# A mixture-of-experts layer whose router runs once per quarter of the positions, with a region of rows for each expert

## The chip, the cores and the metric

The kernel runs on one core of one Trainium2 chip. A core has five engines that run at the same time, each with an instruction queue of its own: TensorE (PE; its weight loads are shown as PEld), VectorE (DVE), ScalarE (ACT), GpSimd (POOL) and SyncE (SP), and 16 DMA engines that they share. The metric is the device time of one execution in microseconds. The kernel before took 1349.56 us (median of three runs, 1344.41 to 1350.19).

## The reference, cut to what matters

The input `x` has 16 sequences of 256 positions and 128 channels, 4096 rows in all. Four layers follow each other, each on the layernorm of `x` and added to `x`:

```python
x = x + attn_a(layernorm(x))   # 16 heads of 8, within blocks of 64 positions of a sequence
x = x + ffn(layernorm(x))
x = x + attn_b(layernorm(x))   # 16 heads of 8, over the 16 sequences at each position
x = x + ffn(layernorm(x))

def ffn(x):                                  # the same weights both times
    logits = flat_x @ Wr                     # 8 experts
    top_vals, top_idx = jax.lax.top_k(logits, 2)
    rw = softmax(top_vals)
    combine = sum(rw[..., None] * one_hot(top_idx, 8), axis=1)
    g, u = einsum('nc,ech->neh', flat_x, Wg), einsum('nc,ech->neh', flat_x, Wu)
    eo = einsum('neh,ehc->nec', silu(g) * u, Wd) * DEPTH_SCALE   # hidden 512
    return einsum('ne,nec->nc', combine, eo)
```

So each row needs just two of eight experts. Which two, and how many rows an expert gets, is known only at run time.

## The kernel before, in words

**Tiling.** The 256 positions are cut into four quarters of 64 (`NQ`), each held on chip as a tile `xq[q]` of 128 partitions by 8 groups (`NG`) by 128 channels; a group is two sequences. Two quarters make a half (`NH` = 2, `QH` = 2 quarters each): 2048 rows (`TH`), of which each goes to two experts. A *stage* `s` is the expert layer on one half: stages 0 and 1 are the first expert layer on halves 0 and 1, stages 2 and 3 the second.

**Attention.** `attention_a` and `attention_b` work on one quarter: a layernorm with transposes to the channel-major form (`layernorm_t`; its `pow` for the reciprocal deviation is L235, on POOL), queries and keys, and then group by group the scores (L329, L415), the maximum and difference on DVE, the exponential on ACT (L343, L436), transposes, the product with the values (L360, L453) and the division. `attention_a` ends a group with two additions on POOL (L367, L368).

**Router.** `router(s)` takes the two quarters of a half together (16 groups, `GH`). It makes their layernorm, which is kept in `rows` along with the weight and the destination of each row (132 numbers of 4 bytes), the logits, the two largest of eight (`largest`), the weights, and then the place of each row among the rows of its expert: a running sum over the groups, products with a triangle and with ones (`rank`, `count`). The number of rows of each expert in the half is rounded up to tiles of 256 (`TT`), from `over` to `base`; an expert's rows begin where the tiles of the expert before end. `of_i` says for each of 23 tiles (`NT`) which expert it belongs to. Finally 32 indirect DMAs on POOL (L621), one for each group and choice, scatter 128 rows each to their places in `sorted_in[s]` in DRAM, which has 5888 rows.

**Fill.** Since no expert fills its last tile, `sorted_in[s]` is first written with zeros whose destination is out of the way (`fill`, one DMA on ACT's queue for each stage, L210).

**Experts.** `experts()` walks over 4 x 23 tiles. `fetch` reads the tile's 256 rows (`xin`) from fixed places of `sorted_in[s]`, loads the expert's number into a register of SP and reads its three weight matrices with it. A tile is two steps (pairs of hidden chunks): products L719 for `g` and `u`, tanh on ACT (L724), two operations on DVE (L725, L727), the product back (L670) one step later, and at the end the transposes (L681), the scaling by the row's weight on ACT (L686, `y`), the destination on DVE (L691, `to`) and two indirect DMAs on POOL (L693) that scatter 256 result rows into `results[s]`. `xin`, `w`, `y` and `to` have three buffers each. Rows that no one filled get a destination behind all real rows: `to` is the smaller of the destination read and a constant of the tile, `pads`.

**Combine.** `combine(s)` reads the results of a half back in order and adds them to `xq` (L747, L753).

**What sets the order.** The program writes `attend("a", 0)` (both quarters' attention and the router of stage 0) first, then the fills of stages 1 to 3, then the stages. In stage `s` the tiles' 46 steps are written interleaved with `beside(s)`: the combine of the stage before, then attention on the other half and its router. `rate` says how many steps of the side are written after each step of the tiles; the divisor 0.8 makes the side end after 80% of them. `ROUTER`, `STEPS_A`, `STEPS_B` count the side's steps. This written order is a priority: a planner places each instruction on its engine's queue, earlier written ones first, with later ones where an engine would stand idle. On the chip each queue then runs in its order.

Of the kernel before, what the change touches and what calls it, by code (L numbers as in the profile page):

```python
# [10 lines left out]
F32 = mybir.dt.float32  # L11
# [8 lines left out]
P = 128  # L20
# [8 lines left out]
CH = 512  # L29
# [20 lines left out]
K_ONE, K_TRI, K_STEP, K_LOW, K_NUM, K_DEST, K_PAD, K_END = 204, 332, 460, 468, 532, 556, 588, 634  # L50
# [4 lines left out]
def _constants():  # L55
# [28 lines left out]
    c[:, K_PAD : K_PAD + 2 * NT] = pad.reshape(P, 2 * NT)  # L84
    return c
# [3 lines left out]
def hybrid_kernel(  # L89
# [23 lines left out]
    p2 = ctx.enter_context(tc.tile_pool(name="p2", bufs=2))  # L113
    p3 = ctx.enter_context(tc.tile_pool(name="p3", bufs=3))
# [71 lines left out]
    number = k_sb[0:1, K_NUM : K_NUM + NT]  # L186

    rows = [const.tile([P, GH, TOP, RW], F32, name=f"rows{i}") for i in range(1)]
    for t in rows:
        nc.gpsimd.memset(t[:, :, :, C + 1 : RW], 0.0)  # L190
        nc.gpsimd.tensor_copy(
            t[:, :, :, C + 1],
            k_sb[:, K_DEST : K_DEST + TOP * GH].rearrange("p (g k) -> p g k", k=TOP),
        )

    runs = [const.tile([P, NG + GH, NE], F32, name=f"runs{i}") for i in range(2)]
# [3 lines left out]
    sorted_in = [dram.tile([NT * TT, RW], F32, name=f"sorted_in{s}") for s in range(NS)]  # L200
# [4 lines left out]
    nc.gpsimd.memset(zero[:, C + 1 : C + 2], float(TOP * TH + NT * TT))  # L205
# [3 lines left out]
    def fill(s):  # L209
        done = nc.scalar.dma_start(  # L210
            out=sorted_in[s].rearrange("(n p) r -> p n r", p=P),
            in_=zero.unsqueeze(1).to_broadcast([P, NT * TT // P, RW]),
        )
        before[s] = done.ins

    fill(0)

# [267 lines left out]
    def router(s):  # L485
        hf, layer = s % NH, s // NH + 1
        n = f"F{layer}{hf}"
        row = rows[0]
        pl = psum(f"lg_{n}")
        for qq in range(QH):  # L490
            q = QH * hf + qq
            lnT = p1.tile([P, TQ], F32, tag="lnF", name=f"ln_{n}_{qq}")

            def put(half, pt):
                nc.scalar.copy(lnT[:, half * CH : (half + 1) * CH], pt)

            def keep(g):
                return row[:, qq * NG + g, 0, 0:C]

            yield from layernorm_t(q, f"{n}_{qq}", put, keep)  # L500
            for g in range(NG):
                gg = qq * NG + g
                nc.tensor.matmul(
                    pl[:, gg * NE : (gg + 1) * NE],
# [337 lines left out]
```

## Time and profile before

| | |
|---|---|
| median of three runs | 1349.56 us |
| the profiled execution's own time | 1348.74 us |
| its span, first to last instruction | 1346.9 us |
| mean granted TensorE clock | 0.816 |
| PE / weight loads / DVE / ACT / POOL busy | 79% / 58% / 49% / 28% / 29% |
| DMA | 132.97 MB, 99 GB/s on the mean |
| first tile's first product (L719) | 278.67 us |
| first tanh of stages 1, 2 and 3 | 592.9, 886.4 and 1186.9 us |

The profile is of one execution. Times in it count from the first instruction. A line of a group says the code line, engine, operation and what it writes and reads (out<-in), then the busy time, the mean of one in ns, and the idle time just before, with what ended it. A line of the timeline gives start and duration in us, then the same, with the idle time in brackets. "ACTq" or "SPq" is the engine's sequencer, which issues DMAs. The granted clock is a share of TensorE's full speed.

### The profile page before, as it was taken

The page shows a single profiled execution, that of the slowest core. Times are in us where ns is not written, and L with a number is a line of the kernel's source. Part 1 is how long each engine was busy: PE and PEld are TensorE (multiplying, and loading weights), DVE is VectorE, ACT ScalarE, POOL GpSimd, SP SyncE. Part 2 cuts the span into 40 slices and gives each one's busy share as a digit, 9 for nine tenths or more (in the row PEclk, how much of TensorE's full clock was granted, in tenths as well). Part 3 has the DMA queues.
Part 4 walks back from the last instruction along what each step waited for, and adds up shares of the span by engine and source line. Part 5 has one row for each costly group of instructions (what it writes and reads, how often), then busy time and mean ns, then how long its engine had stood idle before and what let it go on. Part 6 is the DMA issues. An engine that isn't in the chain of part 4 may idle for free.

```text
span 1346.9 us, 22348 instructions
## 1 busy us (share of the span) xinstructions
PE 1059.1 (79%) x8280; PEld 775.2 (58%) x8280; DVE 655.1 (49%) x1760; ACT 377.3 (28%) x789; POOL 385.8 (29%) x461
## 2 busy tenths in 40 slices
PE   2798995079999998187999985578999985499992
PEld 0565665056766676063675763455766764378882
DVE  3435444045566645047657662157557651255443
ACT  0212221022333332022333431123333421133441
POOL 1001003712222214724112127423121127432331
PEclk9556555588898989586999997688899988699996
DMA  9900000321232323242332332261231332276563
GB/s 251 211 1 1 1 1 17 109 65 61 85 93 65 95 64 105 81 146 77 92 93 73 96 110 80 91 207 41 81 109 63 99 93 82 89 226 215 187 188 105
DMA packets 140635, 132.97 MB, mean 99 GB/s; under 512 B 12016, under 2 KB 111856, under 8 KB 140528
## 3 DMA queue, kind: packets, MB, share of 16 engines
q1 hardware_dynamic: 105920, 97.79, 24.5%
q0 software_dynamic: 9984, 20.73, 4.6%
q10 hardware_dynamic: 24624, 13.03, 4.5%
q8 instruction: 66, 1.08, 0.3%
q14 instruction: 41, 0.34, 0.1%
HBM read 96.26 MB, written 35.24 MB: 98 GB/s over the span
## 4 chain that ended last, share of the span: by engine, by line
PE 54%; another core or an unknown queue 6%; DVE 5%; POOL 4%; DMA 4%; issue 4%; ACT 2%; SPq 0%; ACTq 0%; POOLq 0%; DVEq 0%
PE g L719 11%; PE u L719 11%; PE acc L670 10%; PE sc_A L329 3%; PE sc_B L415 3%; POOL sorted_in L621 2%; PE o_A L360 2%; PE o_B L453 2%; DMA results<-yo,to 2%; PE xt L662 2%; PE y L681 2%; PE t_A L349 1%; PE t_B L442 1%; PE v_B L275 1%
## 5 line engine op out<-in xcount | busy, mean ns | idle before, releaser
L693 POOL DMA_INDIRECT results<-yo,to x184 | 178.2, 969 | 513.5 <-ACT yo L686 480.0
L719 PE MATMUL g<-xT,w 128*128 128x256 f32 x736 | 220.1, 418 | 39.0 <-issue 38.1
L670 PE MATMUL acc<-h,w 128*128 128x256 f32 x736 | 209.1, 403 | 25.3 <-DVE h L727 25.0
L725 DVE SCALAR_TENSOR_TENSOR th<-th,g 128x512 f32<-128x512 f32 x184 | 125.6, 683 | 201.7 <-ACT th L724 122.6
L719 PE MATMUL u<-xT,w 128*128 128x256 f32 x736 | 212.7, 409 | 2.1 <-DVE th L725 2.1
L724 ACT ACTIVATE th<-g 128x512 f32<-128x512 f32 x184 | 109.9, 597 | 341.4 <-PE g L719 212.9
L719 PEld LDWEIGHTS g<-xT,w 128*128 128x128 f32 x736 | 143.1, 205 | 82.4 <-issue 62.9
L670 PEld LDWEIGHTS acc<-h,w 128*128 128x128 f32 x736 | 141.1, 201 | 57.0 <-DVE h L727 34.4
L727 DVE TENSOR_TENSOR h<-th,u 128x512 f32<-128x512 f32 x184 | 125.8, 684 | 76.3 <-PE u L719 27.2
L719 PEld LDWEIGHTS u<-xT,w 128*128 128x128 f32 x736 | 142.2, 205 | 27.4 <-issue 5.1
L621 POOL DMA_INDIRECT sorted_in<-rows,pos_i_F x128 | 122.8, 959 | 44.2 <-issue 37.2
L329 PE MATMUL sc_A<-kA,qA 32*64 32x256 f32 x512 | 108.5, 537 | 16.5 <-DVE ex_A L337 15.2
L360 PEld LDWEIGHTS o_A<-va,eT_A 128*64 128x64 f32 x1024 | 79.4, 181 | 30.2 <-ACT eT_A L353 15.9
L336 DVE TENSOR_REDUCE mx_A<-sc_A 128x4 f32<-128x256 f32 x128 | 51.4, 420 | 89.7 <-PE sc_A L329 87.9
L367 POOL TENSOR_TENSOR att_A<-att_A,bv_bc 128x128 f32<-128x128 f32 x32 | 14.5, 452 | 250.7 <-DVE att_A L296 238.4
L360 PE MATMUL o_A<-va,eT_A 128*64 128x18 f32 x1024 | 85.5, 244 | 0.1
L662 PE MATMUL xt<-k_sb,xin 128*128 128x128 f32 x184 | 40.5, 306 | 52.6 <-DMA xin<-sorted_in 47.8
L681 PE MATMUL y<-k_sb,yT 128*128 128x128 f32 x184 | 39.5, 299 | 48.6 <-ACT yT L678 40.0
L678 ACT COPY yT<-acc 128x256 f32<-128x256 f32 x92 | 34.2, 372 | 154.5 <-PE acc L670 128.5
L686 ACT ACTIVATE yo<-y,xin 128x128 f32<-128x128 f32 x184 | 57.1, 364 | 69.8 <-PE y L681 58.8
L681 PEld LDWEIGHTS y<-k_sb,yT 128*128 128x128 f32 x184 | 24.2, 150 | 65.8 <-ACT yT L678 44.4
L691 DVE TENSOR_TENSOR to<-xin,k_sb 128x2 int32<-128x2 f32 x92 | 14.9, 162 | 96.0 <-DMA results<-yo,to 50.9
(134 smaller groups left out, 1238.5 us busy)
## 6 DMA issues: line engine op xcount, KB each, us to landing
w<-in_wg SPq DMA_DIRECT2D x92, 256.0 KB
w<-in_wu SPq DMA_DIRECT2D x92, 256.0 KB
w<-in_wd SPq DMA_DIRECT2D x92, 256.0 KB
sorted_in<-zero ACTq DMA_DIRECT2D x4, 3036.0 KB
xin<-sorted_in SPq DMA_DIRECT2D x92, 132.0 KB
back<-results SPq DMA_DIRECT2D x16, 512.0 KB
results<-yo,to POOLq DMA_INDIRECT x184
xq<-in_x SPq DMA_DIRECT2D x8, 256.0 KB
```

What stands on the lines that cost most here:

```text
L329: nc.tensor.matmul(sc[b * BS : (b + 1) * BS, 0 : 4 * BS], lhsT=qT[rows, blocks[b]], rhs=kx[rows, :, blocks[b]], start=True, stop=True,)
L360: nc.tensor.matmul(po[b * BS : (b + 1) * BS, i * 18 : (i + 1) * 18], lhsT=eT[:, i, b * BS : (b + 1) * BS], rhs=vt[:, b, 2 * i : 2 * i + 2, ...
L621: put_row = nc.gpsimd.indirect_dma_start(out=sorted_in[s], out_offset=bass.IndirectOffsetOnAxis(ap=pos_i[:, k, g : g + 1], axis=0), in_=ro ...
L662: nc.tensor.transpose(pt[:, b * P : (b + 1) * P], t[:, b, 0:C], ident)
L670: nc.tensor.matmul(acc[:, 0:TT], lhsT=w[:, 2, hc * P : (hc + 1) * P], rhs=h[:, j * TT : (j + 1) * TT], start=(hc == 0), stop=(hc == NHC - 1),)
L681: nc.tensor.transpose(py[:, b * P : (b + 1) * P], yT[:, b * P : (b + 1) * P], ident)
L686: nc.scalar.activation(y[:, b, :], py[:, b * P : (b + 1) * P], AF.Identity, scale=t[:, b, C : C + 1],)
L693: put_row = nc.gpsimd.indirect_dma_start(out=results[s], out_offset=bass.IndirectOffsetOnAxis(ap=to[:, b : b + 1], axis=0), in_=y[:, b, :] ...
L719: nc.tensor.matmul(p[:, j * TT : (j + 1) * TT], lhsT=w[:, k, hs], rhs=xT, start=True, stop=True,)
L724: nc.scalar.activation(th, pg, AF.Tanh, scale=0.5)
L725: nc.vector.scalar_tensor_tensor(th, th, 1.0, pg, ALU.add, ALU.mult)
L727: nc.vector.tensor_tensor(h, th, pu, ALU.mult)
```

## The change

Each expert gets a region of its own of 2048 rows (`TH`, as many as a half can send to one expert) in `sorted_in`, which now has 16,384 rows and is there once for each half, not for each stage. A row's place is the region's start plus its place among the rows of its expert, so it no longer depends on how many rows the other experts get, and a quarter can scatter its rows as soon as it is through its own router; `ends` carries the counts from the first quarter to the second. `router(s, qq)` handles one quarter (8 groups, 16 scatters), and `attend` calls it right behind the attention of that quarter. After the second quarter, `tile_tables` works out for each tile the expert, the row at which it begins (read by SP into a register) and from which of its rows on nothing new was written (`behind`). Rows there may be left from two stages before; `to` is now the larger of the destination and `behind`. The regions are filled once, at the start, and the scatters of stages 2 and 3 follow the reads (`before`) of stages 0 and 1. `y` and `to` get six buffers, `rows` two tiles of half the size. The divisor of `rate` goes from 0.8 to 0.6.

```diff
-    rows = [const.tile([P, GH, TOP, RW], F32, name=f"rows{i}") for i in range(1)]
+    rows = [const.tile([P, NG, TOP, RW], F32, name=f"rows{i}") for i in range(QH)]
...
-    sorted_in = [dram.tile([NT * TT, RW], F32, name=f"sorted_in{s}") for s in range(NS)]
+    sorted_in = [dram.tile([NE * TH, RW], F32, name=f"sorted_in{i}") for i in range(NH)]
...
-    def fill(s):
+    def fill(hf):
         done = nc.scalar.dma_start(
-            out=sorted_in[s].rearrange("(n p) r -> p n r", p=P),
-            in_=zero.unsqueeze(1).to_broadcast([P, NT * TT // P, RW]),
-        )
-        before[s] = done.ins
+            out=sorted_in[hf].rearrange("(n p) r -> p n r", p=P),
+            in_=zero.unsqueeze(1).to_broadcast([P, NE * TH // P, RW]),
+        )
+        before[hf] = [done.ins]
 
     fill(0)
+    fill(1)
...
-    def router(s):
+    tables, ends = {}, {}
+
+    def router(s, qq):
+        hf = s % NH
+        q, n = QH * hf + qq, f"F{s}_{qq}"
+        row = rows[qq]
...
-        while by < GH:
+        while by < NG:
...
+        start = first_row if qq == 0 else ends[s, qq - 1]
+        ends[s, qq] = p2.tile([P, NE], F32, tag="end", name=f"end_{n}")
+        nc.vector.tensor_tensor(ends[s, qq], start, pn[:, 0:NE], ALU.add)
+        place = p1.tile([P, NG, NE], F32, tag="place", name=f"place_{n}")
+        nc.vector.tensor_tensor(
+            place, rank.rearrange("p (g e) -> p g e", e=NE),
+            start.unsqueeze(1).to_broadcast([P, NG, NE]), ALU.add,
+        )
...
+        for g in range(NG):
+            for k in range(TOP):
+                put_row = nc.gpsimd.indirect_dma_start(
+                    out=sorted_in[hf],
+                    out_offset=bass.IndirectOffsetOnAxis(ap=pos_i[:, k, g : g + 1], axis=0),
+                    in_=row[:, g, k, :], in_offset=None,
+                )
...
+                follow(put_row.ins, before[hf])
+                after.setdefault(s, []).append(put_row.ins)
+            yield
+        if qq == QH - 1:
+            before[hf] = []
+            yield from tile_tables(s, ends[s, qq])
+
+    def tile_tables(s, end):
...
+        count = small("count", [P, NE])
+        nc.vector.tensor_tensor(count, end, first_row, ALU.subtract)
...
+        at = small("at", [P, 2, NE])
+        nc.vector.tensor_tensor(at[:, 0], base, count, ALU.add)
+        nc.vector.tensor_tensor(at[:, 1], first_row, base, ALU.subtract)
+        rise = small("rise", [P, 2, NE - 1])
+        nc.vector.tensor_tensor(rise, at[:, :, 1:NE], at[:, :, 0 : NE - 1], ALU.subtract)
...
+        tab_i = p2.tile([1, 2, NT], I32, tag="tab_i", name=f"tab_i_{s}")
+        nc.vector.tensor_copy(tab_i, tab)
         yield
...
+        behind = p2.tile([P, NT, 2], F32, tag="behind", name=f"behind_{s}")
+        nc.vector.tensor_tensor(
+            behind, pads, stop.unsqueeze(2).to_broadcast([P, NT, 2]), ALU.is_ge
+        )
+        nc.vector.tensor_tensor(behind, behind, pads, ALU.mult)
+        tables[s] = tab_i, behind
...
             t = p3.tile([P, 2, RW], F32, tag="xin", name=f"xin_{n}")
+            row = nc.values_load(
+                tables[s][0][0:1, 1, i : i + 1], engines=[SP], min_val=0,
+                max_val=NE * TH - TT,
...
-                in_=sorted_in[s][i * TT : (i + 1) * TT].rearrange("(p b) r -> p (b r)", b=2),
+                in_=sorted_in[s % NH][bass.ds(row, TT)].rearrange("(p b) r -> p (b r)", b=2),
             )
             follow(got.ins, after[s])
+            before[s % NH].append(got.ins)
...
-                y = p3.tile([P, 2, C], F32, tag="y", name=f"yo_{n}")
+                y = p6.tile([P, 2, C], F32, tag="y", name=f"yo_{n}")
...
-                to = p3.tile([P, 2], I32, tag="to", name=f"to_{n}")
-                nc.vector.tensor_tensor(to, t[:, :, C + 1], pads[:, i], ALU.min)
+                to = p6.tile([P, 2], I32, tag="to", name=f"to_{n}")
+                nc.vector.tensor_tensor(to, t[:, :, C + 1], tables[s][1][:, i], ALU.max)
...
     def attend(kind, hf):
-        for q in range(QH * hf, QH * hf + QH):
-            yield from (attention_a if kind == "a" else attention_b)(q)
-        yield from router((0 if kind == "a" else NH) + hf)
+        for qq in range(QH):
+            yield from (attention_a if kind == "a" else attention_b)(QH * hf + qq)
+            yield from router((0 if kind == "a" else NH) + hf, qq)
...
-    ROUTER = 3 * QH + 4 + GH // 4
+    ROUTER = QH * (6 + NG) + 3
...
     for _ in attend("a", 0):
         pass
-    for s in range(1, NS):
-        fill(s)
     main = experts()
...
-        rate, due = STEPS[s] / (0.8 * 2 * NT), 0.0
+        rate, due = STEPS[s] / (0.6 * 2 * NT), 0.0
```

## The prediction

> **What bounds the kernel now.** I read the share of each engine first, then the granted clock by slices, then tables by stage, then the timeline where the tables showed a hole. The page says that no one engine is full over the whole span: PE is busy for 79%, POOL for 29%. The table of stretches (us, then busy time and instructions of PE, weight loads, DVE, ACT and POOL, then the clock, the DMA share and GB/s) says where PE is missing:
>
> ```profile
> 46.00:212.00 166.00, 150.38 (x1003) 102.27 (x1004) 70.56 (x236) 38.06 (x52) 16.28 (x32) 0.52 0.11 24
> 234.00:278.00 44.00, 0.46 (x2) 0.29 (x2) 0.17 (x2) 0.00 (x0) 30.30 (x32) 0.50 0.35 111
> ...
> 540.00:580.00 40.00, 9.09 (x24) 6.73 (x25) 2.75 (x4) 2.57 (x7) 25.90 (x28) 0.55 0.23 70
> 630.00:795.00 165.00, 155.30 (x2084) 113.44 (x2083) 108.09 (x276) 63.11 (x132) 31.59 (x31) 0.99 0.29 87
> 815.00:863.00 48.00, 19.42 (x60) 14.41 (x58) 4.71 (x7) 4.04 (x10) 32.54 (x34) 0.66 0.23 72
> 1112.00:1157.00 45.00, 18.24 (x65) 13.70 (x63) 5.60 (x9) 5.24 (x12) 34.23 (x36) 0.73 0.24 76
> 1187.00:1316.00 129.00, 124.95 (x617) 108.06 (x616) 66.76 (x118) 51.41 (x132) 42.02 (x44) 1.00 0.65 198
> ```
>
> The reader is to see two kinds of stretch. Where attention runs beside the tiles (630 to 795), or tiles run alone (1187 to 1316: 23 tiles in 129 us, 5.6 us a tile), PE is busy for 94 to 97%: there only PE's work counts. In four others PE is nearly still while POOL issues its 32 scatters: 234 to 278 and one hole in each of the stages 0, 1 and 2. The groups give the price of one scatter, and who waits behind it:
>
> ```profile
> L693 POOL DMA_INDIRECT results<-yo,to x184 | 178.2, 969 | 513.5 <-ACT yo L686 480.0
> L621 POOL DMA_INDIRECT sorted_in<-rows,pos_i_F x128 | 122.8, 959 | 44.2 <-issue 37.2
> ```
>
> A scatter takes 0.96 us and 0.30 us of issue: 1.26 us, so 32 take 40.4 us. The timeline of stage 1 shows why the tiles stop meanwhile (start, us, instruction, idle before it and what ended that):
>
> ```profile
> 821.24 0.60 ACT L724 ACTIVATE th<-g 128x512 f32<-128x512 f32 x1 [3.46 <-PE u L719]
> ...
> 851.66 0.95 POOL L621 DMA_INDIRECT sorted_in<-rows,pos_i_F  x1 [0.31 <-issue]
> 852.92 0.96 POOL L693 DMA_INDIRECT results<-yo,to  x1 [0.30 <-issue]
> ...
> 856.29 0.69 DVE L727 TENSOR_TENSOR h<-th,u 128x512 f32<-128x512 f32 x1 [19.69 <-issue]
> ...
> 863.32 0.60 ACT L724 ACTIVATE th<-g 128x512 f32<-128x512 f32 x1 [17.09 <-remote]
> ```
>
> The results of finished tiles (L693) stand in POOL's queue behind the router's scatters. Tiles `y` and `to` have three buffers, so the fourth tile has none, and DVE and ACT wait. The wait's name ("issue", "remote") doesn't say so. What says so is that DVE moves 3.4 us after the first L693 was issued. Last, the start of the trace (ACTq issues a DMA, ACT computes):
>
> ```profile
> 22.01 12.18 ACTq L210 DMA_DIRECT2D sorted_in<-zero  x1
> 34.23 0.69 ACT L263 ACTIVATE kT_A<-k_A,b_sb 128x512 f32<-128x512 f32 x1 [11.64 <-issue]
> 34.29 11.90 ACTq L210 DMA_DIRECT2D sorted_in<-zero  x1
> ...
> 46.24 2.00 ACT L343 ACTIVATE ex_A<-ex_A 128x1024 f32<-128x1024 f32 x2 [10.74 <-DVE mx_A L336]
> ```
>
> A fill's issue holds ACT until the fill before it has drained (12 us for 5,888 rows). Also, these fills stand behind the whole first attention in the code and run here at 22 us: instructions are ordered by a planner, which lets later work go early where an engine is idle.
>
> **The change, part by part.** The profiled execution took 1348.74 us (span 1346.9 and 1.8 around it), 0.8 under the median of 1349.56; the sum is made against it.
>
> *Opening (0 to 278).* (a) Before the first tile all 32 scatters lie open, 233.4 to 273.8, and PE does nothing. Afterwards the first quarter's 16 are issued beside the second quarter's attention and 16 remain: 16 x 1.26 = -20.2. The first quarter's 20.2 us on POOL is passed by the adds of attention (L367, L368). Attention has two `att` buffers and took 166 us for 16 groups, 10.4 a group, so it can run 20.8 us ahead of POOL: no cost, and up to 20 if this cover goes. The second quarter's layernorm (L235 on POOL) ran at 19.47 us already, long before any scatter. (b) The chain from the last addition (213.3) to the first scatter (233.4) loses the five operations from `over` to `base` (1.4 us) and one doubling (0.25), and some 14 operations of 0.29 go to half their size (the 128x64 ones of L578 take 0.22): -2.5; ends 0 and -3.5. (c) A second router now stands between the two attentions, mostly under the second's work: +3; ends 0 and 18, its whole chain. (d) The two fills have 16,384 rows each, in place of four of 5,888, and both precede attention in the code. Fills drain at 12.0 us for 5,888 rows, so the first, slowed by the loads of x as now, is through at about 44 us, and fill 1 holds ACT until then. ACT's first copy (20.98 now) goes to 44, the first exp (46.24 now, since its input is ready at 42.3 but ACT isn't) to about 58: +12. Ends: -10, if nothing is held and the present 11.6 and 10.7 fall away too, and +43, if fill 1 holds ACT until it has drained itself; the first fill's own issue took 0.39 us, which is nearer to the middle. Opening: -20.2 - 2.5 + 3 + 12 = -7.7.
>
> On (d) the Trainium skill says otherwise. In "DMA: Bandwidth & Descriptors", section "Issuing engines are not separate DMA queues", the time that a sequencer needs to start a DMA is called usually small beside the DMA. By that the fills would hold ACT for nothing and (d) would stand at its lower end. The row of 12.18 us decides against it.
>
> *Stages 0 to 2.* (e) The holes: the tanh of one tile follows the last after 40.0 us (539.91 to 579.91), 42.1 (821.24 to 863.32), 38.6 and 13.3 (1117.83, 1156.40, 1169.65), in place of 5.6. That loses 34.4 + 36.5 + 40.7 = 111.6, all behind bursts of 32 scatters. (f) In their place come six bursts of 16, 20.2 us each. Now a burst of 40.4 costs about 36.5, so 4 are absorbed; six buffers of `y` and `to` absorb three tiles more, 3 x 5.6 = 16.8. 4 + 16.8 is just above 20.2, but results add 2.5 us of POOL per tile: +3 for each second quarter's burst, when tiles run alone, and nothing for the first quarter's, when a tile takes over 11 us. +9; ends 0 and 6 x 16. (g) In a stage the router's DVE operations go from 35 to 2 x 26 and 22 for the tables. At 0.2 each for the small ones that is 15.4 us for 9. DVE is busy for 65% beside attention, so part is hidden: +4 a stage, +12; ends 0 and 30. PE gets three more small products, 1 us at most. (h) The rate goes from 0.8 to 0.6: attention is written beside 27.6 steps (half tiles) instead of 36.8, and 9.2 steps more run alone, 2.8 us each. If PE's work simply adds up this moves nothing. If attention is a chain of a length of its own, 9.2 x 2.8 = 25.8 a stage is lost; if it slows the tiles beside it in proportion (240 us for 300 to 540, where 20 tiles at 5.43 and attention's 75, half of the 150 that it took at clock 0.52, make 184: 1.3 times), 7 are won. PE's 94 to 96% is nearest to the first: +3 a stage, +9. (i) In stage 0 POOL's adds of attention stand behind the first quarter's burst: a group takes over 12 us there, two buffers cover 24: +2; ends 0 and 20. Stages: -111.6 + 9 + 12 + 9 + 2 = -79.6.
>
> Costed at nothing: one more register load per tile on SP (SP issues five DMAs in a tile of 5.6 us, each 0.3 to 0.5; when SP is full it costs 0.5 a tile); the weights, whose expert is known some 5 us later (under 15 us of scatters in the opening; without that cover 5, once); the new wait of a stage's scatters for the reads of two stages ago, which ended a stage earlier (what is queued behind it on POOL are the results, at whose end a tile waits); the table `behind`, on DVE beside scatters. The stall at the head of stages 1 and 2 (593 to 630) waits for the last results and stays.
>
> Sum: 1348.7 - 7.7 - 79.6 = 1261.4; 0.8 for the median gives 1262.
>
> A rule of the Trainium skill speaks against two bursts in place of one. "TensorE: Matmul & The Clock Gate", "Why this matters for your kernels", warns of idle gaps of PE above some 3 us, after which the clock falls to half. The trace agrees for gaps (0.55 in 540 to 580) and not for busy stretches: 0.52 from 46 to 212 with PE busy for 91%. As an estimate from that page, each of six gaps would cost a window of 3.4 us at half rate, 10 us in all, in place of (f)'s 9.
>
> **The rivals.** *Scatters still stop the tiles* (slower). If buffers aren't what stops them, or the queue's order sets 16 scatters ahead of several tiles' results, each of six bursts costs its 20.2: 121 in place of 9, 1374. It turns the sign when a burst costs over 17 (6 x 17 - 9 = 93). For it: xin has three buffers still, and DVE stands for 19.69 us in the hole for a reason that the trace doesn't name. Against: L727 resumed just behind L693. 0.09. *Attention is a chain*: (h) at 25.8 a stage, 1262 + 68 = 1330. For it: PE's busy time takes in stalls of matmuls. Against: 94 to 96%. 0.12. *Fill 1 holds ACT till its own end*: (d) at 43, 1293. 0.10. *Nothing moves*: the planner puts the first quarter's scatters beside the second's. Then 32 remain together, the opening gains nothing (1348.7 + 12 + 3 - 2.5), the holes lose only three tiles of 5.6 each (-50), and (g), (h) stay (+21): 1333. For it: a planner may delay what nobody needs. Against: it let fills go early. 0.05.
>
> **How the numbers follow.** My forecast, 0.64, has its own range of 1215 to 1295: (f) and (h) at their good ends and ACT unheld at the lower one, (g) at 30 and (c) at 18 at the upper. With the chain's lower part and the fill, 1213 to 1325 leaves out the slower rival, the upper half of the chain and of "nothing moves", and a little below. 0.5% (7 us) is about what the measurement can tell. Faster: 0.64 + 0.11 + 0.10 + 0.01, taken as 0.85; slower 0.10; the rest 0.05.
>
> **What would show it.** Right: 16 scatters, about 20 us, between the last attention and the first tile; the holes gone, tiles of 5.6 us to the end of each stage; two groups of 16 L621-like scatters a stage; ACT idle to about 44 us. Wrong: tanh spacing over 15 us behind either burst; PE under 85% beside attention; ACT held beyond 60 us; the first quarter's scatters issued together with the second's.

## The result, and the profile after

The change made the kernel slower: 1420.66 us median (1401.92 to 1431.82, four runs) against 1349.88 (1344.41 to 1355.48) beside it, a ratio of 1.044 (95% interval 1.032 to 1.056). Two of the four runs, the longest, at a mean granted clock of 0.786 and 0.787 where the others had 0.804 and 0.792, are left out of the ratio. The prediction said 1262. The profiled execution took 1401.92 us, span 1400.1, so it is 53.2 us longer than the profiled one of before. Later sets of runs fell on other chips, and in two of these sets the kernels behaved otherwise; that is a main finding, told below. Everything in this section but the table at its end comes from the chip of the result.

The table of stretches of the kernel after (us, then busy time and instructions of PE, weight loads, DVE, ACT and POOL, clock, DMA share, GB/s):

```profile
55.00:236.00 181.00, 154.17 (x1006) 103.01 (x999) 81.05 (x280) 37.06 (x53) 34.33 (x50) 0.53 0.18 41
260.00:282.00 22.00, 0.00 (x0) 0.00 (x0) 4.02 (x20) 0.00 (x0) 15.45 (x16) 0.50 0.15 49
...
674.00:736.00 62.00, 50.58 (x575) 38.12 (x574) 36.17 (x129) 16.18 (x37) 14.16 (x19) 0.83 0.19 58
749.00:766.00 17.00, 4.21 (x74) 2.46 (x72) 1.92 (x5) 0.97 (x3) 10.27 (x11) 0.61 0.36 98
855.00:871.00 16.00, 0.61 (x3) 0.19 (x1) 1.38 (x2) 0.84 (x2) 12.34 (x13) 0.61 0.20 65
1246.00:1375.00 129.00, 126.20 (x614) 109.28 (x613) 68.43 (x117) 51.40 (x131) 42.61 (x45) 0.99 0.64 197
```

Attention in the opening (first line) is nearly as before: PE busy for 85% where it was 91% (the first quarter's router now lies in the stretch), clock 0.53. One burst of 16 lies open (second line), half of the old 44 us. Tiles alone still take 5.6 us (last line: 23 in 129). The end of the first quarter's attention and the router behind it, with no burst in the stretch, fill PE beside tiles for 82% only (third line, 50.58 of 62) at a clock of 0.83, where before had 94% and 0.99 beside attention; the low part is its last 20 us, with PE busy for 11.59. And PE still stands beside the bursts: 4.21 us busy of 17, and 0.61 of 16, while POOL is busy. The scatters' groups have kept their price:

```profile
L745 POOL DMA_INDIRECT results<-yo,to x184 | 177.8, 966 | 582.0 <-ACT yo L738 548.5 <-issue 16.1 <-DVE h L779 13.7
L598 POOL DMA_INDIRECT sorted_in<-rows,pos_i_F x128 | 124.3, 971 | 44.1 <-issue 36.3 <-DVE pos_i_F L592 2.8 <-DVE tiles L627 2.8
```

The timeline of PE behind the two bursts of stage 1 shows that this is no wait of the old kind. POOL issues 20 scatters in a row from 736.9 to 762.3 and again from 846.0 to 871.0:

```profile
749.86 0.32 PE L282 MATMUL v_B<-wi,xt 128*32 128x32 f32 x12
...
751.78 0.19 PE L282 MATMUL v_B<-wi,xt 128*32 128x32 f32 x1 [1.22 <-issue]
753.87 0.21 PE L282 MATMUL v_B<-wi,xt 128*32 128x32 f32 x1 [1.91 <-issue]
754.61 0.21 PE L282 MATMUL v_B<-wi,xt 128*32 128x32 f32 x1 [0.53 <-issue]
...
765.14 1.10 PE L282 MATMUL v_B<-wi,xt 128*32 128x32 f32 x36 [0.45 <-issue]
```

```profile
853.72 1.03 PE L722 MATMUL acc<-h,w 128*128 128x256 f32 x4
854.58 1.03 PE L771 MATMUL g<-xT,w 128*128 128x256 f32 x4
871.18 0.69 PE L733 MATMUL y<-k_sb,yT 128*128 128x128 f32 x2 [15.58 <-issue]
```

In the first, PE slows behind the tenth scatter: 36 small products run in 1.10 us once the streak is over; during it they come one in 0.7 to 2.8 us, and the profile names nothing that they wait for ("issue"). In the second PE issues its last product when seven or eight scatters have begun, and the next one 0.1 us behind the end of the last scatter. DVE and ACT stand meanwhile because PE does.

The opening of the kernel after, ACT (ACTq issues a DMA):

```profile
6.05 34.40 ACTq L216 DMA_DIRECT2D sorted_in<-zero  x2
40.49 1.28 ACT L316 ACT_TABLE_LOAD   x1 [40.49 <-issue]
41.78 1.07 ACT L316 COPY lnA<-lnp_A 128x512 f32<-128x512 f32 x2
...
54.60 1.06 ACT L350 ACTIVATE ex_A<-ex_A 128x1024 f32<-128x1024 f32 x1 [5.78 <-DVE ex_A L344]
```

The view joins the two fills' issues: the first takes 0.41 us, the second begins at 16.17 and takes 24.29. It holds ACT to 40.5 us; the first exp is at 54.60 in place of 46.24. By the first tanh of each stage the time went as follows (kind A and kind B of chip are explained with the experiments; "flat" is the kernel of four edits there):

| us | opening | stage 0 | stage 1 | stage 2 | stage 3 to the end |
|---|---|---|---|---|---|
| before, kind A | 280.8 | 312.1 | 293.5 | 300.5 | 160.0 |
| after, kind A | 287.7 | 321.8 | 312.3 | 318.8 | 159.5 |
| after with copies for scatters, kind A | 290.0 | 292.4 | 299.3 | 287.5 | 161.9 |
| flat, kind A | 254.4 | 282.6 | 292.9 | 294.7 | 160.3 |
| before, kind B | 278.4 | 292.5 | 274.2 | 275.2 | 160.8 |
| after, kind B | 285.4 | 309.1 | 262.1 | 262.6 | 160.4 |
| flat, kind B | 256.1 | 276.8 | 250.6 | 250.3 | 162.2 |

### The profile page after: what moved, and what is told of

It reads as the page before. It is cut to its first block, busy times and chain, and to the rows that moved or that the text cites. A ratio compares the mean times of both kernels' runs of the same rounds, so it can differ in the third digit from the quotient of the medians.

```text
span 1400.1 us, 22875 instructions
## 1 busy us (share of the span) xinstructions
PE 1095.0 (78%) x8304; PEld 806.2 (58%) x8304; DVE 677.1 (48%) x1916; ACT 376.8 (27%) x793; POOL 388.2 (28%) x466
## 4 chain that ended last, share of the span: by engine, by line
PE 55%; another core or an unknown queue 6%; DVE 6%; issue 5%; DMA 3%; ACT 3%; POOL 2%; SPq 1%; ACTq 0%; POOLq 0%; DVEq 0%
PE g L771 11%; PE acc L722 10%; PE u L771 10%; PE sc_A L336 3%; PE sc_B L422 2%; PE o_A L367 2%; PE o_B L460 2%; PE y L733 2%; DMA back<-results 2%; PE xt L714 1%; PE v_B L282 1%; PE t_A L356 1%; PE t_B L449 1%; PE lg_F L509 1%
## 5 line engine op out<-in xcount | busy, mean ns | idle before, releaser
L722 PE MATMUL acc<-h,w 128*128 128x256 f32 x736 | 213.4, 410 | 14.7 <-DVE h L779 14.4
L722 PEld LDWEIGHTS acc<-h,w 128*128 128x128 f32 x736 | 145.3, 205 | 42.1 <-DVE h L779 18.6
L336 PE MATMUL sc_A<-kA,qA 32*64 32x256 f32 x512 | 111.9, 534 | 15.6 <-DVE ex_A L344 11.3
L733 PE MATMUL y<-k_sb,yT 128*128 128x128 f32 x184 | 39.8, 301 | 41.1 <-issue 27.3
L336 PEld LDWEIGHTS sc_A<-kA,qA 32*64 32x64 f32 x512 | 33.3, 168 | 47.4 <-issue 33.7
L350 ACT ACTIVATE ex_A<-ex_A 128x1024 f32<-128x1024 f32 x32 | 33.8, 1055 | 93.5 <-DVE ex_A L344 93.5
```

Source lines behind the costliest of these rows:

```text
L336: nc.tensor.matmul(sc[b * BS : (b + 1) * BS, 0 : 4 * BS], lhsT=qT[rows, blocks[b]], rhs=kx[rows, :, blocks[b]], start=True, stop=True,)
L722: nc.tensor.matmul(acc[:, 0:TT], lhsT=w[:, 2, hc * P : (hc + 1) * P], rhs=h[:, j * TT : (j + 1) * TT], start=(hc == 0), stop=(hc == NHC - 1),)
L733: nc.tensor.transpose(py[:, b * P : (b + 1) * P], yT[:, b * P : (b + 1) * P], ident)
```

## The experiments

The theory that I began with, after the result: *PE starves*, POOL's scatters without a pause slow PE itself. Its rival is the one that the prediction was built on: *full buffers*, a tile stands because its results wait in POOL's queue.

The kernel before took 1348.9, 1348.4 and 1348.8 us in the first, second and fifth set of runs and 1283.3 and 1277.3 in the third and fourth; each set had a chip of its own. I call the first kind A (the result's own 1349.88 is like it) and the second kind B. Times of one set are compared with before in that set.

### First set (kind A): buffers, spacing, the fill

Six buffers in the kernel before, and nothing else:

```diff
+    p6 = ctx.enter_context(tc.tile_pool(name="p6", bufs=6))
...
-                y = p3.tile([P, 2, C], F32, tag="y", name=f"yo_{n}")
+                y = p6.tile([P, 2, C], F32, tag="y", name=f"yo_{n}")
...
-                to = p3.tile([P, 2], I32, tag="to", name=f"to_{n}")
+                to = p6.tile([P, 2], I32, tag="to", name=f"to_{n}")
```

> The kernel before, with six buffers of y and to in place of three, and nothing else. Two theories of the holes. 'Full buffers' (the one that the prediction was built on): a tile stands still because it finds no y or to, so three more buffers let three more tiles of 5.6 us through in each of the three holes: 3 x 16.8 = 50 less, about 1299 us. 'PE starves': while POOL issues scatters without a pause, PE itself slows down after some 8 of them, whatever the buffers: the holes stay at 34 to 41 us lost and the time at 1349 within 7.

Measured: 1340.72 us (1329.44 to 1341.79), 0.990 of before (0.983 to 0.997). The tanh spacings over the holes are 42.1, 41.4 and 38.4 us where they were 40.0, 42.1 and 38.6. Three more buffers let no tile through: on this chip buffers didn't end the tiles, and a premise of my step (f) falls.

The scatters spaced. The router puts them on a list, and the loop over half tiles takes one pair from it each time:

```diff
+                if beat:
+                    follow(put_row.ins, beat[-1:])
...
+        for g in range(NG):
+            if s == 0:
+                put_pair(g)
+                yield
+            else:
+                later.append((put_pair, g))
...
+                beat.append(nc.vector.tensor_tensor(h, th, pu, ALU.mult).ins)
...
             next(main)
+            if later:
+                put_pair, g = later.pop(0)
+                put_pair(g)
```

> The kernel after, with the router's scatters of stages 0 to 2 taken two at a time, each pair behind the gated product of the half tile beside which it is written, so that POOL has at most some 4 to 8 in a row in place of 20. 'PE starves': the breaks behind the six bursts (about 17 us each, 100 in all) go, except where a streak of over 8 is left: 1300 to 1330 us. 'Full buffers': six buffers were already there and no tile came to the end of them beside the first quarter's bursts, so only the second quarters' three breaks could shrink: 1350 to 1400. If it is the scatters' traffic or POOL's time as such, it is the same in sum, spread thinner: 1390 to 1410.

Measured: 1363.89 us (1348.87 to 1384.84), 1.008 of before (1.003 to 1.012), where the kernel after stands at 1.044; 34 to 64 us more than I expected. Spacing helps, not as much as it should if only long streaks cost something; but streaks of 10 and 12 were left behind the second quarters.

Pauses in the burst:

```diff
+            if s > 0 and g % 2 and g < NG - 1:
+                for _ in range(4):
+                    rest = nc.gpsimd.tensor_copy(row[:, :, 1, 0:C], row[:, :, 0, 0:C])
+                rested = [rest.ins]
...
-                follow(put_row.ins, before[hf])
+                follow(put_row.ins, before[hf] + rested)
```

> The kernel after, with four idle copies of 1.06 us on POOL behind every fourth scatter of a burst (stages 0 to 2): the same scatters, POOL busy 12.7 us longer in each burst and waiting some more for landings, but never more than 4 to 6 scatters in a row. 'PE starves' by unbroken streaks: PE gets its pause, the breaks shrink although POOL works longer: 1310 to 1360 us. 'Full buffers', or POOL's time as such: each of six bursts lasts 13 to 20 us longer and so does its break: 1480 to 1520.

Measured: 1367.67 us (1358.31 to 1394.76), 1.012 of before (1.002 to 1.022). POOL is busy for 464.9 us in place of 388.2, and the kernel is faster than the one without pauses. Behind the second quarters' bursts the tiles now follow each other after 8.9, 6.0 and 5.8 us (stage 1), where they took 11.8 and 16.6; behind the first quarters' the two slow ones are 26.3 and 20.4 in place of 31.8 and 16.5, together the same. POOL's time as such is excluded as the cause: it grew. The order of its queue isn't excluded by this run, since results now pass between the groups (behind the second quarters they stand in streaks of 6 to 10 with four of the router's scatters in each).

The second fill on SP:

```diff
-    def fill(hf):
-        done = nc.scalar.dma_start(
+    def fill(hf, engine):
+        done = engine.dma_start(
...
-    fill(0)
-    fill(1)
+    fill(0, nc.scalar)
+    fill(1, nc.sync)
```

> The kernel after, with the second fill issued by SP, behind the loads, in place of ACT. If it was the second fill's issue that held ACT to 40.5 us, ACT's first copy goes to some 20 to 30 us, the first exp from 54.6 to about 46, and the opening loses 8 to 13: about 1388 to 1393. If the traffic of the fills holds the opening (the loads of x and of the weights beside them), nothing is won: 1401.

Measured: 1375.20 us (1357.15 to 1403.23), 1.012 of before (1.006 to 1.017). The timeline of ACT in this kernel:

```profile
5.51 0.41 ACTq L216 DMA_DIRECT2D sorted_in<-zero  x1
...
12.51 0.59 ACT L316 COPY lnA<-lnp_A 128x512 f32<-128x512 f32 x1 [5.28 <-PE lnp_A L254]
...
25.21 1.06 ACT L350 ACTIVATE ex_A<-ex_A 128x1024 f32<-128x1024 f32 x1 [5.50 <-DVE ex_A L344]
```

The issue takes 0.41 us, the first copy goes from 41.78 to 12.51, the first exp from 54.60 to 25.21 and the first tile from 287.7 to 257.1: 30 us, not 13. The first fill holds nobody; what holds ACT is the second's issue behind the first, and the kernel before paid for the same thing. The Trainium skill, "DMA: Bandwidth & Descriptors", section "Issuing engines are not separate DMA queues", calls the time that an issue takes on its engine usually small beside the DMA and sees no more than that to be won by another engine; here that time was 24.29 us for the second fill, and the measurement decides.

### Second set (kind A): what in a scatter stops PE

Plain copies in place of the scatters, and scatters of 16 bytes in place of 528. Both read stage 0's rows in the later stages, and give results their places in order:

```diff
+        if s > 0:
+            for i in range(18):
+                busy = nc.gpsimd.tensor_copy(row[:, :, 1, 0:C], row[:, :, 0, 0:C])
+                follow(busy.ins, [cast.ins] + before[hf])
...
-                in_=sorted_in[s % NH][bass.ds(row, TT)].rearrange("(p b) r -> p (b r)", b=2),
+                in_=sorted_in[0][bass.ds(row, TT)].rearrange("(p b) r -> p (b r)", b=2),
...
+                    nc.vector.tensor_scalar(to, pads[:, i], -float(TOP * TH), None, ALU.add)
```

> The kernel after, with each burst of 16 router scatters in stages 0 to 2 replaced by 18 plain copies of 1.06 us on POOL, one after another (some 20 us, as long as the burst). It leaves out the sorting of stages 1 to 3: their tiles read the rows sorted for stage 0, and write their results in order. The results' scatters wait in POOL's queue as before. If scatters themselves slow PE, the six breaks (about 17 us each) shrink to a few us: 1300 to 1340 us. If it is the queue's order or POOL's time, the breaks stay: 1390 to 1410.

```diff
-                    out=sorted_in[hf],
+                    out=sorted_in[hf] if s == 0 else thin,
...
-                    in_=row[:, g, k, :], in_offset=None,
+                    in_=row[:, g, k, :] if s == 0 else row[:, g, k, 0:4], in_offset=None,
...
+    thin = dram.tile([NE * TH, 4], F32, name="thin")
```

> The kernel after, with the router's scatters of stages 0 to 2 writing 16 bytes a row in place of 528, into a table of their own; it leaves out the sorting of stages 1 to 3 in the same way as the kernel with copies. The same number of scatters, of rows, and the same time on POOL, 33 times fewer bytes. If issuing scatters without a pause is what slows PE, the breaks stay: 1385 to 1410. If the bytes do it, they go: 1300 to 1340.

Measured: 1332.88 us with copies, 1419.71 with narrow scatters, one run each, before 1348.36. The two bursts of stage 1, first in the kernel with copies, then in that with narrow scatters (columns as above):

```profile
718.00:734.00 16.00, 13.72 (x148) 7.87 (x148) 12.70 (x16) 4.91 (x10) 15.04 (x16) 1.00 0.33 105
...
819.00:838.00 19.00, 17.26 (x81) 14.06 (x80) 14.88 (x29) 6.39 (x16) 17.82 (x18) 0.98 0.50 157
```

```profile
747.00:780.00 33.00, 20.45 (x170) 11.89 (x168) 11.92 (x27) 5.43 (x10) 17.16 (x18) 0.69 0.20 50
857.00:888.00 31.00, 13.60 (x51) 11.11 (x51) 7.19 (x19) 3.92 (x9) 19.44 (x21) 0.68 0.29 83
```

POOL is busy for 15 to 19 us in each of the four lines. Beside copies PE has 13.72 of 16 and 17.26 of 19 us; beside scatters of a thirty-third of the bytes 20.45 of 33 and 13.60 of 31 (up to the bursts' ends at 769 and 880 it is 12.57 of 22 and 8.71 of 23). So it is the indirect scatter itself that slows PE, not its bytes and not POOL's being busy. The order of the queue is not quite the same in the two: at most eight copies stand between two results, where up to ten scatters did. That the order isn't the cause rests on six buffers above, and on the fourth set, where the kernel after runs with its own order and PE goes on. The copies also size it: stages 0 to 2 take 879.2 us (292.4 + 299.3 + 287.5) in place of 952.9, so the router's scatters cost the kernel after some 74 us; against the kernel with narrow scatters, which ran beside it and leaves out the same, it is 81 (960.5).

The rate back at 0.8, and the first quarter's router written between the steps of the second attention:

```diff
-        rate, due = STEPS[s] / (0.6 * 2 * NT), 0.0
+        rate, due = STEPS[s] / (0.8 * 2 * NT), 0.0
```

> The kernel after with the rate back at 0.8. The prediction gave the change of the rate 3 us a stage. If it costs more, through the head of stages 1 and 2, where a tile stands 40 us in place of 31.6 since more of attention is written ahead of it: -17 for the two heads, -5 more for mixed tiles that are closer together; 1375 to 1390. If work only adds up: 1395 to 1411. Against a gain: the second quarter's burst then lies in the last tiles of a stage, and where it ends behind them the next stage waits: up to +15 a stage.

```diff
-        for qq in range(QH):
-            yield from (attention_a if kind == "a" else attention_b)(QH * hf + qq)
-            yield from router((0 if kind == "a" else NH) + hf, qq)
+        attention, s = attention_a if kind == "a" else attention_b, (0 if kind == "a" else NH) + hf
+        yield from attention(QH * hf)
+        first = router(s, 0)
+        for i, _ in enumerate(attention(QH * hf + 1)):
+            yield
+            if i % 3 == 2 and next(first, True) is None:
+                yield
+        yield from first
+        yield from router(s, 1)
```

> The kernel after, with the first quarter's router written between the steps of the second quarter's attention, one step of it behind every third of attention's, and its PSUM buffer taken only behind the layernorm. If the router's chain of small steps between two attentions is what the prediction mis-sized in (c) and (g), the gap between the quarters in the opening falls from 37 to 20 to 25 us, and the slow tile ahead of each first burst from 24 to about 15: -12 to -17 and three times -9; 1360 to 1380. If it is DVE's work as such, it is only moved: 1395 to 1411.

Measured: the rate 1382.80 us (1375.28 to 1387.00), 1.025 of before (1.018 to 1.031); the merged router 1364.34 (1355.66 to 1382.52), 1.008 of before (1.003 to 1.012). With the rate back, the standing tile at the head of stages 1 and 2 takes 35.0 and 35.8 us in place of 39.8 and 40.1, half of the way back to before's 31.6; stages 1 and 2 gain 3 and 9 us, and stage 0, which has no such head, 19 (321.8 to 302.5). With the merged router the gap between the quarters' exps in the opening falls from 37.3 to 25.7, as expected, but the second and third gap behind it grow from 7.5 and 10.1 to 13.7 and 16.0, so the opening keeps 2 us of the 12. In stages 1 and 2 the slow tile ahead of the first burst goes from 23.8 to 19.1, less than expected, and the burst behind it is broken up (12 in a row in place of 20). The merging moved most of the router's work rather than hid it; how much of its gain (1.008 for 1.044) is the broken streak isn't told apart.

### Third set (kind B): the edits together

The fill on SP, the merged router, the spaced scatters and the rate 0.7, called flat. In the opening a pair follows an exp:

```diff
-            nc.scalar.activation(ex, ex, AF.Exp)
+            beat.append(nc.scalar.activation(ex, ex, AF.Exp).ins)
```

> The kernel after with four edits together: the second fill issued by SP; the first quarter's router between the steps of the second quarter's attention; the scatters of all stages taken in pairs, one pair for each half tile and behind its product (in the opening behind an exp); the rate 0.7. If what the single edits showed is the whole cause and adds up: -30 (fill), -45 to -70 (scatters no longer stop PE), -10 to -20 (router's chain and rate) from 1402, so 1280 to 1320. If the scatters' stops only gave way to another bound, as PE's work or attention's chain: 1330 to 1360.

The same with a ramp, rate 0.75:

```diff
-        rate, due = STEPS[s] / (0.6 * 2 * NT), 0.0
-        for _ in range(2 * NT):
+        slow = 12 if 0 < s < NS - 1 else 0
+        rate, due = (STEPS[s] - slow) / (0.75 * 2 * NT - slow), 0.0
+        for step_no in range(2 * NT):
...
-            due += rate
+            due += rate if step_no >= slow else 1.0
```

> The same with the rate 0.75 and with one step of the side work for each half tile, for the first 12 half tiles of stages 1 and 2. If the 40 us in which the third tile of these stages stands are its place in the written order, behind a chain of small steps (landing, layernorm, query, key) that it needn't wait for, five or six tiles pass in them: -15 to -25 for each of two stages against the flat one. If PE is in need there: the same time as the flat one within 7.

The kernel before with its later fills on SP:

```diff
-        done = nc.scalar.dma_start(
+        done = (nc.sync if s else nc.scalar).dma_start(
```

> The kernel before, with its second to fourth fill issued by SP in place of ACT. If it is the issue that holds ACT, the 11.64 and 10.74 us for which ACT stood still go, the first exp moves from 46.2 to about 25, and the opening loses 20: 1325 to 1332. If something else is late next (the loads of x): 1340 to 1349.

Measured, beside before at 1283.31: flat 1192.93 us (1183.84 to 1200.80), 0.930 (0.926 to 0.935); ramp 1194.49 (1179.73 to 1196.85), 0.927 (0.920 to 0.934); before with fills on SP 1275.36 (1269.64 to 1286.39), 0.995 (0.991 to 0.998). The flat kernel beats both kernels. The ramp did what it should at the head (the next tiles of stage 1 follow after 5.6, 9.8, 12.0 and 7.7 us where one took 36.4), and gave all of it back later (25.2 and 27.5 us at two tiles), as it would if PE's work adds up. The fills won before 8 us, not 20: its first exp comes at 32.0, where the kernel before has 43.1 on a chip of this kind, and its first scatter only 7 us earlier (224.1 for 231.2). The later fills' issues now hold SP, for 10.89 and 12.46 us.

What I hadn't expected stood in the flat kernel's trace: streaks of 30 scatters with tiles of 5.6 us beside them. That put the theory in doubt; the next set is about it.

### Fourth set (kind B): the kernels again

> The kernel after, unchanged, once more beside the kernel before, since the kernel before took 1349 us on the chips of the first two sets of runs and 1283 us on that of the third, where 30 scatters in a row did not slow PE. If PE's stops behind some 10 scatters belong to a chip and not to the program: on a chip like the third the ratio is 0.93 to 0.99, as the prediction's sum (1262 of 1349, 0.935) has it less the 29 us of the opening that the fills took; on one like the first two it is 1.03 to 1.05 again. If they belong to the program: 1.03 to 1.05 on either.

> The kernel before, unchanged, for its trace on the same chip. If PE's stops belong to the chip: where it takes 1283 us, tiles go on behind the start of each burst of 32 until three of them wait for POOL (some 17 us more than in the first trace), and the hole is 28 to 32 us in place of 39 to 42; where it takes 1349 the holes are as in the first trace.

> The kernel before with six buffers of y and to, once more. On a chip where PE goes on during a burst, the buffers are what ends the tiles, and three more of them shrink each of three holes by up to 16.8 us: 1233 to 1250 where before takes 1283. On a chip where PE stops, 1340 to 1349 as in the first set.

> The flat kernel of four edits once more. On a chip like the third 0.93 of before again. On a chip like the first two its second quarters' scatters and results still make streaks of 30 beside tiles alone, so PE would stop there for some 10 to 25 us in each of three stages: 1270 to 1320 where before takes 1349.

Measured, all four unchanged kernels: after 1278.94 us (1249.34 to 1284.09) beside before at 1277.33 (1269.40 to 1282.75). Three of the four runs of after lie at 1276 to 1284 and one at 1249, so no difference can be told; before in its profiled run 1283.00; six buffers 1256.89; flat 1197.79. The second burst of stage 1 in the kernel after, POOL with 28 scatters in a row:

```profile
711.00:735.00 24.00, 23.36 (x304) 14.79 (x303) 18.31 (x44) 10.46 (x18) 18.47 (x19) 0.98 0.42 128
...
798.00:832.00 34.00, 32.52 (x155) 28.11 (x155) 17.40 (x39) 12.79 (x32) 25.55 (x27) 0.96 0.72 212
```

PE is busy for 32.52 of 34 us beside 27 of them (second line) and for 23.36 of 24 beside 19 in the first quarter's burst: on this chip PE doesn't stop. The hole of the kernel before in stage 1 here, its burst beginning at 782:

```profile
785.00:806.00 21.00, 21.00 (x103) 18.27 (x103) 9.69 (x15) 8.34 (x20) 15.96 (x17) 0.96 0.53 159
806.00:831.00 25.00, 2.11 (x7) 1.50 (x6) 0.76 (x2) 0.89 (x3) 19.06 (x20) 0.59 0.24 80
```

For 21 us PE is full, four tiles begin, and only then it stands for 25: the buffers end the tiles, as the prediction had it. Six of them bring 20 us against the set's median (one run): the holes of stages 1 and 2 lose 19.1 and 22.2 us where they lost 25.8 and 28.1, some 6 us each and not the 16.8 that I gave three buffers.

### Fifth set (kind A): both remedies on a chip that stops

Flat and after unchanged, and flat with four copies behind each fourth scatter of the second quarters:

```diff
+            if s > 0 and qq == QH - 1 and g % 2 and g < NG - 1:
+                for _ in range(4):
+                    pause = nc.gpsimd.tensor_copy(row[:, :, 1, 0:C], row[:, :, 0, 0:C])
+                paused[:] = [pause.ins]
...
-                follow(put_row.ins, reads)
+                follow(put_row.ins, reads + paused)
```

> The flat kernel of four edits, beside the kernels after and before on one chip. On a chip where PE stops behind some ten scatters (before at 1349 us): three streaks of 30 beside tiles alone stop it, 10 to 25 us each, so 1270 to 1320, 0.94 to 0.98 of before; on one where PE goes on (before at 1280): 0.93 again.

> The flat kernel with four idle copies of 1.06 us on POOL behind each fourth scatter of the second quarters. Where PE stops in streaks, the pauses of 4.2 us keep it going: 1240 to 1290 where before takes 1349, and 15 to 50 under the flat one. Where PE goes on without pauses they only take POOL's time beside tiles alone: the flat one's time within 10.

> The kernel after, unchanged, on the same chip: 1.03 to 1.05 of before where PE stops in streaks, 0.97 to 1.01 where it goes on.

Measured, beside before at 1348.79: flat 1283.51 us (1279.45 to 1288.34), 0.951 (0.944 to 0.958); with pauses 1288.48 (1283.02 to 1300.73), 0.957 (0.948 to 0.965); after 1401.59 (one run). So the result's 1.04 came again on this kind of chip, and flat beats both kernels on either. Pauses add nothing to spacing: behind the second quarters they save some us, and the last scatters come that much later (the stage's last tile takes 12.4 us).

One stretch of the flat kernel in stage 1, the first quarter's scatters spaced beside attention, on kind A and then on kind B:

```profile
676.00:748.00 72.00, 61.63 (x729) 45.48 (x730) 32.37 (x84) 19.82 (x41) 22.99 (x24) 0.79 0.23 68
```

```profile
667.00:714.00 47.00, 46.48 (x728) 35.61 (x727) 31.18 (x81) 19.72 (x41) 22.83 (x24) 1.00 0.34 101
```

The same matmuls (729 and 728) and the same 24 scatters, in groups of two to eight: 72 us on the one, 47 on the other. (72 - 47) / 24 is 1.0 us for each scatter, as an estimate that puts the whole difference down to them: PE stands for 10 of the 25 us and works longer for 15, at a granted clock of 0.79 in place of 1.00. What the lower clock takes and what the scatters take directly isn't told apart. That bends the theory: it isn't the length of the streak alone that costs; beside attention and tiles short groups cost as well. It isn't a price of every scatter either. Ahead of this stretch only the results' pairs are scattered, and the first seven tiles of the stage take 104.6 us on kind A and 103.1 on kind B. In the opening of the kernel after, without tiles, the first quarter's 16 scatters in a row delay one group of attention by 2.9 us (14.1 for 11.2), the next gaps make it good, and from its first exp to its last the second quarter takes 72.2 us there and 71.8 on kind B. Beside tiles alone the pauses do help, as the kernel with pauses showed.

## Why the prediction was wrong, step by step

- **(f) is the step that failed on the chip of the result.** It took six bursts of 16 at 9 us in all, because buffers would absorb them. Measured by the kernel with copies they cost 74, and the reason isn't the one that I worked with: on kind A a scatter slows PE itself. On kind B the step was right in mechanism and near in size in stages 1 and 2: behind the second quarters' bursts tiles follow after 5.6 to 5.9 us, where I had given 3 a burst, and behind the first quarters' after 14.6 and 15.1 where neighbours take 11 to 12, some 3 us each where I had nothing. The rival that I gave 0.09, scatters that still stop the tiles, came true; its turning point of 17 us a burst (16 would have done: 6 x 16 - 9 is 87, the whole gain) is about what each break behind a second quarter cost (19.5, 17.2 and 18.9), for a cause that it left open. The clue was in the profile of before: DVE standing for 19.69 us for a reason that the trace didn't name. I set the coincidence of one L693 above it.
- **(e)**: the holes of 34 to 41 us did go, and what I took for one cause was two. On kind A, PE's slowing lies in them too: the same kernel loses 29.0, 25.8 and 28.1 there on kind B.
- **(g) and (h)** were mis-sized everywhere. With copies, so without the scatters' cost, stages 0 to 2 gain 26.9 us on before (906.1 to 879.2); my terms without (f) gave 88.6. So (g), (h) and (i) took 85 where I had 23, at most, as the copies themselves load DVE (177 us a stage in place of 164). On kind B the holes that went were 82.9 us, and stages 0 to 2 gained 8.1 (841.9 to 833.8): (f) to (i) took 75 in that run in place of 32. The parts that can be read: the head of stages 1 and 2, +8.4 each on kind A, +4.2 and +5.0 on kind B, on kind A half of it by the rate. I had let this stall stay, as a wait for the last results; the ramp, where the next tiles pass in 5.6, 9.8, 12.0 and 7.7 us, shows that the written order makes it. And the slow tile ahead of the first burst of stages 1 and 2, 24 us where neighbours take 11 to 12, on both kinds: the first quarter's router is a chain of small steps between two attentions, and I had costed its DVE time, not its length. Of stage 0 on kind B (+16.6) this is shown: PE is busy for 297 of 309 us, at a granted clock of 0.82 against 0.91 for before, and from 432 to 469 us it is busy without a break at 0.50. At 0.91 the 309 us would be 279, as an estimate, so the clock is enough for the loss; what lowered it stays open. Of four runs of after there the profiled one took 1281.41 at a mean clock of 0.822 and the shortest 1249.34 at 0.844.
- **(c)** likewise: +3 taken, the gap between the quarters grew by 16.9, near the upper end of 18. The merged router shows that 12 of it can be moved, and that most is then paid later.
- **(d)** was right in size (+13.3 at the eighth group for +12) and in mechanism. Its lower end of -10 was too near: without the second fill's issue the eighth group is at 94.4 us where before had 113.2, 19 us earlier.
- **(a) and (b)** were right: 16 scatters in 260.3 to 279.4, and 17 us in place of 20 from the last addition to the first of them. The opening's sum, -7.7 predicted and +6.9 measured, is wrong by (c).
- The rivals "fill 1 holds ACT till its own end" and "nothing moves" didn't come; "attention is a chain" came in part, through the router in it.

On kind B, then, the sum misses by (c), (g), (h) and stage 0, and ends at no change; on kind A (f) adds the rest.

## What to carry to other kernels

Where an engine stands and the profile names no cause but "issue", that is the thing to measure before a sum is built on another: replace the suspected neighbour by plain work of the same length, as the copies did here. Work that is cut into two parts and put between others is costed by the length of its chain, not by its engine's busy time. A DMA that is issued behind a large one on the same engine can hold that engine, here for 24 us, until nine tenths of the first's packets had gone; give it to an engine that has nothing to do, and compare kernels on more than one chip where scatters run beside matmuls.

## What the runs showed of the hardware

- On some chips GpSimd indirect scatters slow PE, and their bytes don't matter (16 or 528 a row): beside attention and tiles, groups of two to eight cost about 1.0 us a scatter, as an estimate from one stretch (72 us for 47, 24 scatters). The results' pairs cost next to nothing there (104.6 us for 103.1 over seven tiles), and so do 16 in a row beside attention alone (72.2 for 71.8). On the other chips none of this shows.
- The five sets fell in two groups with nothing between, before at 1348 to 1349 and at 1277 to 1283 us; that it is the chip, and not something else that went with it, isn't shown. In the traces of kind A no DMA has a time of landing, in those of kind B most have (2.3 to 3.3 us in the median for the scatters). Not all of the difference lies in the bursts: of the 19.3 us that stage 1 of before takes longer on kind A, 10.7 are its hole, and for the rest no run here names a cause.
- On kind A PE runs on for 8 to 14 us of a streak and then takes a small instruction in 0.7 us or a multiple of it, or none, with nothing awaited. No load of instructions ends that: from 837 to 887 us, around the second stop of the kernel after (855.6 to 871.2), the DMA queues that bring instructions (q8 and q14) move no packet. What holds PE stays open.
- One ACT issue of a fill of 16,384 rows behind another took 24 us of the engine (16.17 to 40.46); from SP it cost ACT nothing.
- Attention A in the opening runs at a granted clock of 0.52 to 0.53 with PE busy for 85 to 91%, on both kinds of chip.
